# Layer 3 of a four-layer convolution block: two buffers for a block's v in the projections, and another order of the first key rows' loads

## The chip, the core and the metric

The kernel runs on one core of a Trainium2 chip, and the whole computation is one launch. The metric is the device time in microseconds (us), as the median of several executions. The engines are named as the profile names them: PE is TensorE's matmul side and PEld its weight load, DVE is VectorE, ACT is ScalarE, POOL is GpSimd and SP is SyncE, which here does nothing but issue transfers (DMAs).

## What is computed

The input `x` has 4 images of 256 channels on a 48x48 grid, float32. Four layers follow one another, each of the form "x plus a function of the group-normalised x". Cut to what matters here:

```python
x = x + _L0_conv_ref(_gn(x), ...)   # 7x7 dilated convolution -> softmax over 49 taps -> weighted sum of shifted x
x = x + _L1_conv_ref(_gn(x), ...)   # 3x3 convolution of signs
x = x + _L2_conv_ref(_gn(x), ...)   # 3x3 convolution with ternary weights
x = x + _L3_conv_ref(_gn(x), L3_conv_Wq, L3_conv_Wk, L3_conv_Wv, L3_conv_Wout, L3_conv_bout)

def _L3_conv_ref(x, Wq, Wk, Wv, Wout, bout):      # HEADS = 8, d = 32
    q = einsum('bchw,oc->bohw', x, Wq); k = ...Wk; v = ...Wv      # 1x1 projections, 8 heads of 32
    q = sigmoid(q); k = sigmoid(k)
    v = v / maximum(norm(v, axis=1), 1e-12)                       # per head and position
    ...
    for w in (1, 2, 4):     # windows of 48, 24 and 12 rows and columns round each position
        attn = q . (sum over the window of k v)  /  (q . (sum over the window of k) + 1e-6)
    return Wout . concatenate(outs) + bout
```

So layer 3 is linear attention over three square windows. The kernel computes it as scores (q times k), times a mask for each window, times v.

## The kernel before

The kernel works image by image through layers 0 to 2. Layer 3 cannot begin before image 0 has passed layer 2. Its projections for image 0 are interleaved with the last image's layers 0 to 2, as a "filler"; the attention of layer 3 begins after that. The projections of images 1 to 3 are interleaved with the attention of the image before.

A projection is done by groups: a group is one block of 8 rows (there are NRB = 6 blocks in an image, and NKC = 3 column tiles in a block). This is the part that makes v of a block. `take` and `free` are counters of the program that writes the instructions; they decide the order of instructions, not waits on the chip. Waits on the chip come from the buffers: an instruction that writes a buffer waits until the last user of that buffer is done, and where that user is a transfer, until it has landed. Every engine executes its instructions in the order in which they are written here.

```python
free = {"xr": 2, "xn": 2, "kt": 2, "sq": 2, "vt": 1, "cs": 1, "o": 1, "rc": 2, "res": 2}
...
def v(self, g, a, c):                       # group g, block of rows a, column tile c = 0, 1, 2
    ...
    if c == 0:
        yield from take("vt")
        self.vs[g] = (
            self.scr.tile([P, NKC, HEADS, D], F32, tag="vt", name="vt", bufs=1),
            self.scr.tile([P, NKC, HEADS], F32, tag="ss", name="ss"),
        )
    vt, ss = self.vs[g]
    yield from bank(1)
    ps = self.ps_tile()[:, 0:C].rearrange("p (h d) -> p h d", d=D)
    for ct in range(NCT):
        pe.matmul(ps, self.xn[g][:, ct, c, :], proj["v"][:, ct, :], start=(ct == 0), stop=(ct == NCT - 1))
    self.used(g)
    yield 1
    act.copy(vt[:, c], ps)                  # ACT empties the PSUM bank into vt
    yield 1
    yield from take("sq")
    sq = self.scr.tile([P, HEADS, D], F32, tag="sq", name="sq")
    pool.tensor_mul(sq, vt[:, c], vt[:, c])
    yield 2
    dve.tensor_reduce(ss[:, c, :], sq, AX.X, ALU.add)
    free["sq"] += 1
    if c < NKC - 1:
        return
    ...                                     # 1/norm of each head: ACT square root, DVE reciprocal and a Newton step
    dve.tensor_mul(vt, vt, r...)            # normalised in place
    yield 1
    sync.dma_start(out=v_d[b][:, a * NKC : (a + 1) * NKC], in_=vt)
    free["vt"] += 1
    made.add(("v", b, a))
```

The class `Projection` is used twice: with the pool `scr0` for image 0 (opened with two buffers for each name, and two PSUM tiles), and with the pool `scr` inside layer 3 for images 1 to 3 (also two buffers for each name). `bufs=1` overrides that for `vt`.

```python
def project_first():                        # the filler during the last image's layers 0 to 2
    scr, ps = (first.enter_context(tc.tile_pool(name=name, bufs=2, side="right", **kwargs))
               for name, kwargs in (("scr0", {}), ("ps_0", {"space": PSUM})))
    ...
    groups = [(a, ("k0", "v", "q0")) for a in range(NRB)]
    groups += [(a, ("k1", "q1")) for a in range(NRB)]
    proj["first"] = Projection(0, scr, ps, "ps", [P, 512]), groups
    start(paced(proj["first"][0].groups(groups), 1))
    while active:
        advance()
        yield 1.2
```

Layer 3's attention takes the tiles of keys for one block of query rows in an order that alternates near and far rows. One tile is a pair (block of key rows a, column tile c). The scores of a tile need `ks` of its row block; its sums, written LAG = 2 tiles later, need `vs` of it.

```python
def load_kv(b, ct, a):
    ks = kvp.tile([P, NKC, P], F32, tag="ks", name="ks")
    sync.dma_start(out=ks..., in_=k_d[b][chans, cols])
    vs = kvp.tile([P, NKC, HG, D], F32, tag="vs", name="vs")
    sync.dma_start(out=vs, in_=v_d[b][:, a * NKC : (a + 1) * NKC, ct * HG : (ct + 1) * HG, :])
    kvs[b, ct, a] = ks, vs

def tiles_of(rb):
    tiles = [(a, c) for a in sorted(range(NRB), key=lambda a: abs(a - rb)) for c in (1, 0, 2) if seen(0, a, rb)]
    near = [t for t in tiles if seen(NW - 1, t[0], rb)]
    far = [t for t in tiles if t not in near]
    both = min(len(near), len(far))
    return [t for pair in zip(near, far) for t in pair] + near[both:] + far[both:]
    # for rb = 0: (0,1) (2,1) (0,0) (2,0) (0,2) (2,2) (1,1) (3,1) (1,0) (3,0) (1,2) (3,2)
...
seen_first = HALVES[0] // RB + 1            # 4
until(("q", 0, 0, 0), ...)                  # q, k and v of these rows are written
qs = {0: load_q(*order[0])}
for a in range(seen_first):                 # 0, 1, 2, 3
    load_kv(0, 0, a)
...
for n in range(len(stream) + LAG):          # the attention's main loop, one tile after the other
    ...
        ss = [blocks[i].scores(pr, a, c) for pr in range(NPR)]      # PE, two PSUM tiles of the pool's two
        ahead.append(blocks[i].masked(a, c, ss))                    # DVE, ACT and POOL empty and mask them
    ...
```

The output projection's weights `wout_sb` (768 KB) are loaded once, by a transfer that ACT issues at the beginning of layer 3.

Of the kernel before, what the change touches and what calls it, by code (L numbers as in the profile page):

```python
# [12 lines left out]
F32 = mybir.dt.float32  # L13
# [8 lines left out]
P = 128  # L22
# [52 lines left out]
HEADS, D = 8, 32  # L75
# [4 lines left out]
NKC = W // KC  # L80
# [65 lines left out]
def conv_preact_kernel(  # L146
# [113 lines left out]
    def bank(steps):  # L260

        nonlocal bank_free
        while step < bank_free:
            yield 1
        bank_free = step + steps
# [6 lines left out]
    def take(what):  # L272
        while free[what] == 0:
            yield 1
        free[what] -= 1
# [11 lines left out]
    class Projection:  # L287
# [84 lines left out]
        def v(self, g, a, c):  # L372
            b = self.b
            while g not in self.xn or (c > 0 and g not in self.vs):
                if g in self.left:
                    return
                yield 1
            if c == 0:
                yield from take("vt")
                self.vs[g] = (  # L380
                    self.scr.tile([P, NKC, HEADS, D], F32, tag="vt", name="vt", bufs=1),
                    self.scr.tile([P, NKC, HEADS], F32, tag="ss", name="ss"),
                )
            vt, ss = self.vs[g]
# [3 lines that stand above are left out]
                pe.matmul(  # L388
                    ps,
                    self.xn[g][:, ct, c, :],  # L390
                    proj["v"][:, ct, :],
                    start=(ct == 0),
                    stop=(ct == NCT - 1),
                )
            self.used(g)
            yield 1
            act.copy(vt[:, c], ps)
# [10 lines that stand above are left out]
            n = NKC * HEADS  # L408
            t = ss.rearrange("p k h -> p (k h)")
            r, s, u = (small.tile([P, n], F32, tag=f"{x}{n}", name=x) for x in ("vr", "vs", "vu"))  # L410
            dve.tensor_scalar_max(t, t, 1e-24)
            yield 1
            act.activation(s, t, AF.Sqrt)
            yield 1
            dve.reciprocal(r, s)
            dve.tensor_mul(u, t, r)
            dve.tensor_mul(u, u, r)
            dve.tensor_scalar(u, u, -0.5, 1.5, ALU.mult, ALU.add)
            dve.tensor_mul(r, r, u)
            dve.tensor_mul(  # L420
                vt,
                vt,
                r.rearrange("p (k h) -> p k h", h=HEADS)
                .unsqueeze(3)
                .to_broadcast([P, NKC, HEADS, D]),
# [5 lines that stand above are left out]
# [21 lines left out]
    with (  # L452
# [50 lines left out]
        class Stats:  # L503
# [8 lines left out]
            def end(self, wait):  # L512
                mv = small.tile([P, NCT, 2], F32, tag="gn_mv", name="gn_mv")
                for ct in range(NCT):
                    dve.bn_aggr(mv[:, ct, :], self.st[:, ct])
                m = small.tile([P, NCT], F32, tag="gn_m", name="gn_m")
                v = small.tile([P, NCT], F32, tag="gn_v", name="gn_v")
                r = small.tile([P, NCT], F32, tag="gn_r", name="gn_r")
                wait(1.5)
                ps = ps_st.tile([P, NCT], F32, tag="st", name="gn_ps")  # L520
                pe.matmul(ps, gmat, mv[:, :, 0], start=True, stop=True)
                dve.tensor_copy(m, ps)

                dve.tensor_sub(v, mv[:, :, 0], m)
                dve.tensor_mul(v, v, v)
                dve.tensor_add(v, v, mv[:, :, 1])
                wait(2.5)
                ps = ps_st.tile([P, NCT], F32, tag="st", name="gn_ps")
                pe.matmul(ps, gmat, v, start=True, stop=True)
                dve.tensor_scalar_add(v, ps, GN_EPS)  # L530
                rsqrt(r, v, NCT)
                return m, r
# [848 lines left out]
        with tc.tile_pool(name="wst", bufs=1) as wst:  # L1381
# [18 lines left out]
            for ct in range(NCT):  # L1400
                for k0, k1 in TAPS:
# [3 lines left out]
                    else:  # L1405
                        pool_, tag = {
                            (0, 0): (xp, "x1_0"),
                            (0, 2): (xp, "x1_1"),
                            (1, 0): (wst, "raw1"),
                            (1, 2): (wst, "raw"),  # L1410
                        }[ct, k0]
# [70 lines left out]
    with (  # L1482
# [168 lines left out]
        def load_kv(b, ct, a):  # L1651

            chans, cols = slice(ct * P, (ct + 1) * P), slice(a * NB, (a + 1) * NB)
            ks = kvp.tile([P, NKC, P], F32, tag="ks", name="ks")
            sync.dma_start(out=ks.rearrange("p k n -> p (k n)"), in_=k_d[b][chans, cols])
            vs = kvp.tile([P, NKC, HG, D], F32, tag="vs", name="vs")
            sync.dma_start(
                out=vs, in_=v_d[b][:, a * NKC : (a + 1) * NKC, ct * HG : (ct + 1) * HG, :]
            )
            kvs[b, ct, a] = ks, vs  # L1660

        def load_q(b, ct, rb):
            qs = qp.tile([P, RB, W], F32, tag="qs", name="qs")
            sync.dma_start(
                out=qs.rearrange("p r w -> p (r w)"),
                in_=q_d[b][ct * P : (ct + 1) * P, rb * NB : (rb + 1) * NB],
            )
            return qs
# [158 lines left out]
        def seen(wi, a, rb):  # L1827
            r0, r1 = rows_seen(wi, a, rb)
            return r0 < r1

        def tiles_of(rb):


            tiles = [
                (a, c)
                for a in sorted(range(NRB), key=lambda a: abs(a - rb))
                for c in (1, 0, 2)
                if seen(0, a, rb)
# [5 lines that stand above are left out]
# [84 lines left out]
        seen_first = HALVES[0] // RB + 1  # L1928
        until(("q", 0, 0, 0), *((what, 0, *at) for a in range(seen_first) for what, at in (("k", (0, a)), ("v", (a,)))))
        qs = {0: load_q(*order[0])}  # L1930
        for a in range(seen_first):
            load_kv(0, 0, a)


# [53 lines left out]
        for n in range(len(stream) + LAG):  # L1988
            if n < len(stream):
                i, a, c, at, last = stream[n]  # L1990
# [6 lines left out]
            if n >= LAG:  # L1997
                i, a, c, at, last = stream[n - LAG]
# [57 lines left out]
```

## Time and profile before

| | before |
|---|---|
| time, median of 3 runs (lowest to highest) | 3734.66 us (3732.04 to 3744.95) |
| span of the profiled execution | 3730.0 us |
| granted PE clock, mean | 0.954 |
| instructions | 69121 |

Where these parts lie in the span, with the busy time of the engines in each stretch:

| stretch, us | what runs | PE | DVE | ACT | POOL | PE clock |
|---|---|---|---|---|---|---|
| 1160 to 1300 (140) | last image's layer 0, second half, with image 0's projections | 98.81 | 43.40 | 68.90 | 12.04 | 0.79 |
| 1300 to 1430 (130) | last image's layers 1 and 2, remaining projections, first tiles of layer 3 | 105.89 | 74.55 | 29.29 | 32.17 | 0.90 |
| 1430 to 3050 (1620) | layer 3's attention of images 0 to 2, with projections of images 1 to 3 | 1458.27 | 1132.04 | 579.13 | 1066.85 | 0.97 |
| 3050 to 3730 (680) | the rest of layer 3 | 646.04 | 433.35 | 208.84 | 304.34 | 0.99 |

How to read it. The busy time of an engine beside the length of a stretch tells how near that engine is to setting the pace there; it doesn't tell which wait ends last. In the timeline, one line is a run of like instructions: start, length, engine, operation, then what is written and what is read, and in square brackets the time for which the engine stood idle before it, with the event that ended the idle time. "DMA v_d<-vt" as such an event means that the transfer from `vt` to the scratch tensor `v_d` had landed. A line for "SPq" is the issue of a transfer, not its landing. All lines name L142 because a helper issues every operation, so groups are told apart by the names of their tiles.

### The profile page before, as it was taken

How to read it: one execution, taken by the hardware profiler on the slowest of the kernel's cores; microseconds unless marked ns; L12 is line 12 of the kernel's file. 1: busy time of each engine (PE TensorE's matmuls, PEld its weight loads, DVE VectorE, ACT ScalarE, POOL GpSimd, SP SyncE). 2: the span in 40 equal slices, each digit the busy share in tenths (PEclk: the TensorE clock that was granted, in tenths of full speed). 3: DMA queues.
4: the chain of work that ended last, by engine and by line, in shares of the span. 5: the costliest groups of instructions: out<-in, count | busy, mean ns of one | idle time of the engine just before them, and what ended most of it. 6: DMA issues, size and time to landing. Idle time of an engine off the chain costs nothing. (4 is left out here: it accounts for less than half of the span.)

```text
span 3730.0 us, 69121 instructions
## 1 busy us (share of the span) xinstructions
PE 3284.1 (88%) x26498; PEld 1873.8 (50%) x26498; DVE 2494.9 (67%) x5059; ACT 1067.4 (29%) x2085; POOL 1528.0 (41%) x2184
## 2 busy tenths in 40 slices
PE   3689998998996788988899888999999899999998
PEld 2467686686784664433334333344444344444443
DVE  7876587586583266778667466866577866666665
ACT  0012111111114422443222334333344422333331
POOL 0000120120030024788765476866366766344442
PEclk9789999999997899999899999999999999999999
DMA  7745333324314323345344253434222444200222
GB/s 251 225 143 184 101 108 120 105 98 125 107 65 124 117 70 98 119 140 168 105 133 134 74 151 109 154 99 136 75 94 87 153 124 124 70 31 31 65 60 60
DMA packets 373020, 423.04 MB, mean 113 GB/s; under 512 B 129076, under 2 KB 328532, under 8 KB 371540
## 3 DMA queue, kind: packets, MB, share of 16 engines
q1 hardware_dynamic: 371491, 416.32, 36.2%
q8 instruction: 211, 3.46, 0.4%
q0 software_dynamic: 144, 1.52, 0.2%
q14 instruction: 118, 0.96, 0.1%
q10 hardware_dynamic: 1056, 0.79, 0.1%
HBM read 288.79 MB, written 131.25 MB: 113 GB/s over the span
## 5 line engine op out<-in xcount | busy, mean ns | idle before, releaser
L142 DVE TENSOR_TENSOR sm<-s,masks 128x112 f32<-128x112 f32 (+10 forms) x2592 | 1149.2, 492 | 704.7 <-ACT sm L142 297.1
L142 POOL TENSOR_TENSOR sm<-sm,masks 128x432 f32<-128x432 f32 (+14 forms) x1152 | 883.1, 788 | 900.9 <-ACT sm L142 397.5
L142 ACT COPY sm<-s 128x528 f32<-128x528 f32 (+2 forms) x1152 | 588.3, 534 | 1423.0 <-PE s L142 1281.9
L142 PE MATMUL s<-qs,ks 32*128 32x320 f32 (+3 forms) x5760 | 859.7, 499 | 127.8 <-ACT sm L142 65.2
L142 PE MATMUL acc<-sm,vs 128*32 128x384 f32 (+18 forms) x13440 | 879.5, 384 | 21.5 <-POOL sm L142 21.2
L142 PEld LDWEIGHTS s<-qs,ks 32*128 32x128 f32 x5760 | 372.0, 185 | 558.3 <-DVE sm L142 225.1
L142 PE MATMUL cv<-vx,wt 128*128 128x288 f32 x2080 | 561.1, 426 | 92.5 <-DVE vx L142 50.7
L142 PEld LDWEIGHTS acc<-sm,vs 128*32 128x32 f32 x13440 | 355.0, 110 | 555.0 <-issue 327.0
L142 PEld LDWEIGHTS cv<-vx,wt 128*128 128x128 f32 x2080 | 403.5, 198 | 213.8 <-issue 55.2
L142 POOL MEMSET v<- 128x16 f32 (+1 forms) x120 | 18.5, 214 | 722.1 <-DVE vx L142 628.5
L142 PE MATMUL cv<-v,wl 128*128 128x384 f32 x1152 | 222.2, 352 | 24.3 <-DVE x L142 9.2
L142 PEld LDWEIGHTS cv<-v,wl 128*128 128x128 f32 x1152 | 212.7, 193 | 34.0 <-issue 15.8
L142 POOL TENSOR_TENSOR pt<-pt 128x144 f32<-128x144 f32 x336 | 180.4, 537 | 22.3
L142 POOL TENSOR_TENSOR v<-l2v,v 128x384 fp32r<-128x384 f32 x96 | 109.0, 1164 | 127.0 <-ACT v L142 118.3
L142 POOL TENSOR_TENSOR nhi<-nhi,nq 128x384 f32<-128x384 f32 x144 | 147.9, 1055 | 0.0
L142 PE MATMUL cv<-pad,wl 128*128 128x384 bf16 x864 | 143.1, 327 | 0.0
L142 PE MATMUL out_ps<-o,wout_sb 128*128 128x384 f32 x288 | 123.7, 512 | 11.2 <-DMA rc<-r_d 5.7
L142 DVE TENSOR_TENSOR pt<-cs 128x384 f32<-128x384 f32 x144 | 119.2, 827 | 0.0
L142 PE MATMUL out_ps<-stage,wout_sb 128*128 128x384 f32 x288 | 118.6, 494 | 0.5 <-DVE stage L142 0.5
L142 DVE TENSOR_TENSOR vx<-v 128x868 f32<-128x868 f32 x112 | 115.3, 1055 | 0.5
L142 PE MATMUL proj_ps<-wv_sb,xn 128*128 128x256 f32 x288 | 88.3, 434 | 29.3 <-ACT vt L142 19.3
L142 PEld LDWEIGHTS <-wl 128*128 128x128 bf16 x864 | 83.8, 97 | 59.1 <-issue 0.4
(162 smaller groups left out, 2881.3 us busy)
## 6 DMA issues: line engine op xcount, KB each, us to landing
wt<-wt SPq DMA_DIRECT2D x48, 768.0 KB
kb_d<-pt SPq DMA_DIRECT2D x48, 576.0 KB
rc<-r_d SPq DMA_DIRECT2D x192, 144.0 KB
nhi<-kb_d SPq DMA_DIRECT2D x120, 192.0 KB
nlo<-kb_d SPq DMA_DIRECT2D x88, 192.0 KB
o_d<-stage SPq DMA_DIRECT2D x24, 576.0 KB
o<-o_d SPq DMA_DIRECT2D x24, 576.0 KB
wl<-wl_d SPq DMA_DIRECT2D x16, 768.0 KB
```

The source lines that it names most:

```text
L142: return lambda *args, **kwargs: self.tc.keep_in_program_order(op(*args, **kwargs))
```

## The change

Two edits. The first drops `bufs=1` for `vt`, so that it has its pool's two buffers, in the projections of image 0 and in those of images 1 to 3: a group's first copy into `vt` need no longer wait for the landing of the previous group's transfer out of it. The counter `free["vt"]` stays at 1. The second fetches the first four blocks of key rows in the order in which the first block's tiles use them, 0, 2, 1, 3 where it was 0, 1, 2, 3.

```diff
             if c == 0:
                 yield from take("vt")
                 self.vs[g] = (
-                    self.scr.tile([P, NKC, HEADS, D], F32, tag="vt", name="vt", bufs=1),
+                    self.scr.tile([P, NKC, HEADS, D], F32, tag="vt", name="vt"),
                     self.scr.tile([P, NKC, HEADS], F32, tag="ss", name="ss"),
                 )
@@
         qs = {0: load_q(*order[0])}
-        for a in range(seen_first):
+        for a in dict.fromkeys(a for a, _ in tiles_of(0)):
             load_kv(0, 0, a)
```

## The prediction

> **What bounds the kernel now.** I read the page's first part for the shares, then everything that touches `vt` (the views of that tile), then ACT's and PE's timelines round each wait found there, and last the timeline at the beginning of layer 3.
>
> ```profile
> PE 3284.1 (88%) x26498; PEld 1873.8 (50%) x26498; DVE 2494.9 (67%) x5059; ACT 1067.4 (29%) x2085; POOL 1528.0 (41%) x2184
> ```
>
> PE sets the pace over the whole, so what the change is worth is read from the time for which PE stands still because of the things it touches. The first edit removes only one kind of wait. The view of `vt` in the stretch 1160 to 1430, where image 0 is projected, shows all of it:
>
> ```profile
> L142 ACT COPY vt<-proj_ps x18: 348/372/392, 1162.6 to 1292.4; 128x256 f32<-128x256 f32 x18
>   DMA v_d<-vt: 21.1, 5
>   PEld proj_ps L142: 26.9, 7
>   PE proj_ps L142: 23.2, 5
> ```
>
> Six groups, so five times a group's first copy follows another group's transfer: five waits, 21.1 us in sum. The last two lines are who waited for those copies. The same view for 1430 to 1960 has one idle entry, `PE proj_ps` with 1.1 us, and those for 1960 to 2500 and 2500 to 3050 also show no wait for `v_d`. So in the attention's 18 groups the second buffer has nothing to remove, and the first edit lives from five places. ACT's timeline has them:
>
> ```profile
> 1186.27 0.65 ACT L142 COPY vt<-proj_ps 128x256 f32<-128x256 f32 x2 [5.11 <-DMA v_d<-vt]
> 1204.26 0.65 ACT L142 COPY vt<-proj_ps 128x256 f32<-128x256 f32 x2 [4.18 <-DMA v_d<-vt]
> 1225.13 0.37 ACT L142 COPY vt<-proj_ps 128x256 f32<-128x256 f32 x1 [2.94 <-DMA v_d<-vt]
> 1255.75 0.37 ACT L142 COPY vt<-proj_ps 128x256 f32<-128x256 f32 x1 [1.25 <-DMA v_d<-vt]
> 1283.54 0.37 ACT L142 COPY vt<-proj_ps 128x256 f32<-128x256 f32 x1 [7.61 <-DMA v_d<-vt]
> ```
>
> ACT is busy 68.90 of the 140 us there, so its waits matter only as far as PE stands behind them. PE's timeline of the same places:
>
> ```profile
> 1186.70 2.08 PE L142 MATMUL proj_ps<-wv_sb,xn 128*128 128x256 f32 x4 [6.89 <-ACT vt L142]
> 1204.69 2.07 PE L142 MATMUL proj_ps<-wv_sb,xn 128*128 128x256 f32 x4 [2.48 <-ACT vt L142]
> 1225.91 0.52 PE L142 MATMUL tra<-ident,rows 120*120 120x120 f32 x3 [1.10 <-ACT seen L142]
> 1256.18 1.13 PE L142 MATMUL proj_ps<-wv_sb,xn 128*128 128x256 f32 x4 [0.70 <-ACT vt L142]
> 1283.96 2.08 PE L142 MATMUL proj_ps<-wv_sb,xn 128*128 128x256 f32 x4 [7.28 <-ACT vt L142]
> ```
>
> The second edit is at the beginning of layer 3:
>
> ```profile
> 1416.24 1.66 PE L142 MATMUL s<-qs,ks 32*128 32x384 f32 x8
> 1416.50 0.42 ACTq L1494 DMA_DIRECT2D wout_sb<-in_wout_dram  x1
> 1417.20 0.48 SPq L142 DMA_DIRECT2D ks<-k_d  x1
> 1424.55 1.78 PE L142 MATMUL s<-qs,ks 32*128 32x384 f32 x8 [6.64 <-DMA ks<-k_d]
> ```
>
> The second tile needs row block 2, whose `ks` is the third to be issued (at 1417.20) and is there 7.3 us later. PE stands for 6.64 us, and by then ACT, DVE and POOL have run dry too.
>
> **What the Trainium skill says.** "Perfetto Trace Analysis", Optimization Strategy, says that a bubble that returns on the engine that should be saturated can come from too few buffers. The trace agrees: five waits, each at a group's first copy. "DMA: Bandwidth & Descriptors", Queues, rings and completion order, says that one issuer's descriptors are consumed in ring order and that a DMA engine alternates between issuers' rings by packets. The packet records agree: of the 1536-byte packets (`ks`) row block 1's end at about 1418.4 and row block 2's at about 1423.0, while 512-byte packets (`vs`) and 1024-byte ones (`wout_sb`) run mixed between. So exchanging two loads in SP's ring exchanges their landings. "TensorE: Matmul & The Clock Gate", Part 1, says that PE's clock falls to half after some idle time and returns after sustained work. The trace agrees as far as it goes: the mean granted clock is 0.66 in 1280 to 1300, after the idle 7.28 us, 0.50 in 1415 to 1430 and 1.00 in 1300 to 1332.
>
> **The change part by part.** No instruction is added or removed, and as the counter for `vt` stays at 1, their order is the same but for the two exchanged loads. `vt` takes 3 x 8 x 32 x 4 = 3072 bytes per partition, once more in each of two pools; later tiles of these pools move by that much.
>
> First edit, the five places. I take PE's idle time where the copy ends it, cut to what the landing causes:
> - 1186: the copy could go when ACT is free, at 1181.17 (its exponential from 1180.80 lasts 0.37), as its PSUM tile is full by 1179.8. It comes 5.11 us earlier, and PE, which waits 6.89, gains **5.1**. The matmuls of the last logits stand behind it, so the whole chain of layer 0 moves.
> - 1204: the first v matmuls (start 1200.13, 2.08 us for two copies' worth) fill a bank at about 1201.2, so about 3 of the 4.18 are the landing's; PE idles 2.48, all removed: **2.5**.
> - 1225: PE waits 1.10 for `seen` behind the copy. A round trip from PE to ACT and back is there anyway (0.45 us at 1213.90): I take **0.5**.
> - 1256: **0.7**.
> - 1284: the transfer was issued at 1275.21 behind four weight loads (1270.87 on). The copy also holds up the reciprocal root of layer 1's statistics, at 1285.22 with its input there since about 1277, and the rows of `pad` that layer 1's matmuls need. Layer 1 begins at 1296.39 and moves with it: **7.3**.
>
> Sum 16.1 us. Against it, waits that can step in: ACT's `sg` waits for the landing of `q_d` once for 1.58 us and for 0.38 us, `xn` needs its rows, and `band_d` held DVE's `spread` for 2.1 us. They were hidden in part behind these stalls. I subtract 3 (an estimate: roughly one of these waits again at two of the three big places). **First edit: 13.**
>
> Second edit: row block 2 takes the place of row block 1, so its last packet is at 1418.4 where it was at 1423.0. PE came 1.5 us after the last packet (1424.55), so it would be allowed at about 1420. The scores also need both PSUM tiles emptied: DVE's masks of the first tile run from 1417.98 for 2.28 us, to 1420.26, and ACT's second copy ends at 1419.81. So the scores start at about 1420.3, which is **4.2** us earlier, and the wait left (2.4 us behind DVE) takes the place of the one removed. Row block 1 is then needed by the seventh tile; even at 1424.5 it is there before that. `vs` of row block 2, needed two tiles later, takes the landing of the old `vs` 1 (last packet at about 1422.2), in time.
>
> Clock: shorter idle stretches leave PE less often at half speed. The half-speed stretch from 1281.92 lasts 13.65 us in the trace's clock records, with some 7 us of work in it; the one from 1415.04 lasts 17.07. I add **2**, the vaguest term.
>
> In all 13 + 4 + 2 = 19, and 3734.7 - 19 = 3715.7: I predict **3716 us**.
>
> **The rivals.**
> 1. Another wait takes the place (gain 5 to 10, time 3725 to 3730). ACT has table loads of 1.28 us between its functions in this stretch, two `sg` buffers with transfers of their own, and PE waits 11.4 us for `sg` in 1160 to 1350. For it: these queues are as tight as `vt`. Against it: in each of the three big places the wait was for `vt` alone by 2.5 to 7.3 us, and the transfers that `sg` waits for were issued well before (1183.86, read next at 1194.41).
> 2. The gain is hidden: PE loses it again further on, because the weights of layers 1 and 2 land no earlier. For it: 2.7 MB of weight loads are in flight from 1270.87, at 350 to 430 GB/s. Against it: layer 1's are first in the ring, a quarter of those bytes, some 2 us of traffic, and the start would move only to about 1280. Layer 1 runs with no idle time from 1296.39 for 35.78 us, so from there a shift stays a shift. If true for that place: time about 3723.
> 3. The moved tiles (3 KB further) come to lie on memory that is released later, or the two stretches run at another granted clock. Nothing in the profile speaks for it: the tiles of keys come before the moved pool and the first masks have time. It would cost a few us either way: 3720 to 3737.
>
> **Range and chances.** If rival 1 and 2 both hold, the first edit is worth about 4 and the second 3: 3728. If nothing steps in and the clock gives 6, 16 + 4 + 6 = 26: 3709. The three runs before differ by 13 us, so the range is a little wider on each side: 3705 to 3730. Two per cent are 74.7 us; the whole of the waits concerned is 28 us (21.1 + 6.64). So within 2% is nearly sure: 0.97, faster by more 0.02, slower by more 0.01.
>
> **What would show it.** In the changed profile: no wait of ACT `vt` for `v_d`; layer 1's first long run of `cv` (1296.39 before) at about 1283, which is the first edit's 16 less the 3, give or take the clock; the second tile's scores after an idle time of about 2.4 us that DVE's `sm` ends. From about 1440 on every stage is to have the length it had. The prediction is wrong if the run of `cv` starts after 1290 (then ACT's other waits have stepped in), if the second tile still waits for `ks`, or if the length of the attention from there to the end differs by over 5 us, which neither edit accounts for.

## The result, and the profile after

The changed kernel takes 3714.77 us (median of 4 runs, 3709.3 to 3717.27) where the kernel before took 3737.36 in the runs beside it: a ratio of 0.9936 (95% interval 0.9914 to 0.9958). Measured once more on another chip it is 3715.24 us and 0.9931 (0.9912 to 0.9950). So some 23 to 26 us are gone, within 2%, and near the 3716 us predicted; but the sum behind that number has one term that was far too small, and it lacks a loss that came.

The first line of the page of the changed kernel, busy time by engine: PE's busy time is what it was (3284.1 before), in a span that is 14.5 us shorter in this one execution. That sum hides that PE is faster in one stretch and slower in others; the stretches below tell.

```profile
PE 3283.8 (88%) x26498; PEld 1871.7 (50%) x26498; DVE 2493.9 (67%) x5059; ACT 1067.6 (29%) x2085; POOL 1530.5 (41%) x2184
```

The view of `vt` in image 0's projections, 1140 to 1420: what ended the idle time ahead of its instructions, and who waited for it.

```profile
L142 ACT COPY vt<-proj_ps x18: 350/371/378, 1164.1 to 1272.2; 128x256 f32<-128x256 f32 x18
  ACT vt L142: 100.6, 13
  DVE ss L142: 17.4, 3
  PE proj_ps L142: 2.1, 2
  DVE vr L142: 0.2, 1
...
  PEld proj_ps L142: 9.9, 4
  PE proj_ps L142: 7.3, 2
```

The entry for `v_d` (21.1 us before) is gone. Of the 7.3 us for which PE still waits for a copy, 6.53 are at 1271.69, where ACT first writes layer 1's input (5.86 us at 1291.89 before). PE's timeline of the changed kernel at the places that the prediction went through:

```profile
1182.96 2.07 PE L142 MATMUL proj_ps<-wv_sb,xn 128*128 128x256 f32 x4 [0.73 <-ACT vt L142]
...
1199.23 1.78 PE L142 MATMUL proj_ps<-xn,wk_sb 128*128 128x384 f32 x4 [0.80 <-ACT xn L142]
1200.85 1.45 PE L142 MATMUL proj_ps<-xn,wq_sb 128*128 128x384 f32 x4
1202.14 0.37 PE L142 MATMUL tra<-ident,rows 120*120 120x120 f32 x2
...
1276.97 36.07 PE L142 MATMUL cv<-pad,wl 128*128 128x384 bf16 x216
...
1397.82 1.66 PE L142 MATMUL s<-qs,ks 32*128 32x384 f32 x8
1401.45 2.19 PE L142 MATMUL s<-qs,ks 32*128 32x384 f32 x8 [1.97 <-ACT sm L142]
```

The first line stood at 1186.70 after 6.89 us of idle time. Layer 1's run of `cv` starts at 1276.97 where it was 1296.39. The second tile's scores wait 1.97 us, for ACT's copy, where they waited 6.64 us for `ks`. Two stretches serve from here on. **S1** runs from the second v projection of the second group (1178.68 before, 1180.16 after) to the run of `cv`; **S2** from the first scores to the zeroing matmuls ahead of the first sums. "The rest" is from those to PE's last matmul. The stretches view, S1 before and after (length, then busy us of PE, PEld, DVE, ACT, POOL, then clock, DMA share, GB/s):

```profile
1178.68:1296.39 117.71, 82.50 (x401) 63.16 (x402) 34.38 (x109) 53.41 (x95) 10.26 (x19) 0.77 0.41 128
```

```profile
1180.16:1276.97 96.81, 77.69 (x400) 60.53 (x401) 34.65 (x109) 54.09 (x96) 10.43 (x19) 0.82 0.49 155
```

S1 lost 20.9 us, S2 went from 13.13 to 8.49, and the rest grew from 2295.9 to 2304.5.

### The profile page after: what moved, and what is told of

The parts are those of the page before. It is cut to its first block, busy times and chain, and to the rows that moved or that the text cites. A ratio compares the mean times of both kernels' runs of the same rounds, so it can differ in the third digit from the quotient of the medians.

```text
span 3715.5 us, 69111 instructions
## 1 busy us (share of the span) xinstructions
PE 3283.8 (88%) x26498; PEld 1871.7 (50%) x26498; DVE 2493.9 (67%) x5059; ACT 1067.6 (29%) x2085; POOL 1530.5 (41%) x2184
## 5 line engine op out<-in xcount | busy, mean ns | idle before, releaser
L142 DVE SCALAR_TENSOR_TENSOR x<-cv,alpha,x 128x384 f32<-128x384 f32 x144 | 83.9, 609 | 43.3 <-PE cv L142 43.0
```

The source lines that it names most:

```text
L142: return lambda *args, **kwargs: self.tc.keep_in_program_order(op(*args, **kwargs))
```

## The experiments

All are compared with the kernel before on their own chip. First each edit alone, then the first edit in one of its two pools, then its memory without its effect.

**The first edit alone**

```diff
-                    self.scr.tile([P, NKC, HEADS, D], F32, tag="vt", name="vt", bufs=1),
+                    self.scr.tile([P, NKC, HEADS, D], F32, tag="vt", name="vt"),
```

> The first edit alone (two buffers for vt in both pools, loads in the old order 0, 1, 2, 3). Two stretches are measured in the trace. S1: from the start of the second v projection after 1178 us (before: 1178.68) to the start of layer 1's run of cv (before: 1296.39), 117.7 us before and 96.8 us with the whole change. S2: from the first scores (before: 1416.24) to the zeroing matmuls ahead of the first sums (before: 1429.37), 13.1 us before and 8.5 us with the whole change. Theory (the two edits act apart, each where its own wait was): S1 about 97, S2 about 13, time about 18 us (14 to 21) under before. Rival (the earlier end of layer 2 also changes what is in flight at the start of layer 3): S2 differs from 13.1 by over 2 us.

3711.78 us, ratio 0.9916 (0.9903 to 0.9930). S1 is 90.4, S2 13.4, the rest 2295.2. The edit acts in S1 alone, but takes more than expected: about 28 us between the medians and 31 by the ratio, as much as the whole change or more.

```profile
1186.72:1277.13 90.41, 69.75 (x400) 53.66 (x401) 34.70 (x109) 54.06 (x96) 10.62 (x19) 0.92 0.54 166
```

**The second edit alone**

```diff
-        for a in range(seen_first):
+        for a in dict.fromkeys(a for a, _ in tiles_of(0)):
             load_kv(0, 0, a)
```

> The second edit alone (one buffer for vt, loads in the order 0, 2, 1, 3). Theory: S1 as before, 117 to 118; S2 about 8.5; the second tile's scores wait about 2 us for ACT or DVE and not for ks; time 4 to 5 us under before. Rival (the gain at the start of layer 3 is taken back in the attention, where PE is not the only one that sets the pace): S2 8.5 but time within 1.5 us of before.

3732.85 us, ratio 0.9980 (0.9972 to 0.9988): about 7 us. S1 123.8, S2 8.4, the rest 2291.6, so nothing was taken back. The wait left at the second tile is as long as expected, but is put down to `ks` here, which came about when ACT and DVE were done:

```profile
1431.74 1.94 PE L142 MATMUL s<-qs,ks 32*128 32x384 f32 x8 [2.20 <-DMA ks<-k_d]
```

**Two buffers in image 0's projections only**

```diff
-                    ... tag="vt", name="vt", bufs=1),
+                    ... tag="vt", name="vt", bufs=2 if self.tag == "ps" else 1),
```

> Two buffers for vt in image 0's projections alone; in layer 3's own projections one buffer as before, so no tile of the attention lies elsewhere than before. Theory (the attention's 18 groups have no such wait): as the first edit alone within 3 us, S1 about 97, time about 18 us under before. Rival (the second buffer also matters in the attention, for better or, by moving its tiles, for worse): differs from the first edit alone by over 5 us.

3712.2 us, ratio 0.9925 (0.9912 to 0.9937); S1 92.8, the rest 2295.4. That is the first edit alone within the intervals: no effect of the second buffer shows in the attention's 18 groups.

**One buffer, twice as wide**

```diff
-                    self.scr.tile([P, NKC, HEADS, D], F32, tag="vt", name="vt", bufs=1),
+                    self.scr.tile([P, 2 * NKC, HEADS, D], F32, tag="vt", name="vt", bufs=1)[:, 0:NKC],
```

> One buffer for vt, but twice as wide, its second half unused: the same memory as two buffers, with all tiles where the change has them, and the wait kept. Theory (the wait is what counts): S1 about 117.7, five waits of ACT's copies for v_d, time within 5 us of before. Rival (the gain comes from where the tiles lie, not from the wait): S1 near 97. If moved tiles cost something in the attention, as the 8.6 us by which the one changed profile is longer there could mean, this run is 5 to 9 us slower than before.

3741.12 us, ratio 1.0000 (0.9988 to 1.0012); S1 121.7, the rest 2294.7, and the wait is there in full:

```profile
  DMA v_d<-vt: 23.9, 5
```

With the old order of loads, no effect shows of where the tiles lie.

**One buffer, freed by DVE instead of by the landing**

```diff
-            dve.tensor_mul(vt, vt, r...)
+            vn = self.scr.tile([P, NKC, HEADS, D], F32, tag="vn", name="vn", bufs=1)
+            dve.tensor_mul(vn, vt, r...)
-            sync.dma_start(out=v_d[b][...], in_=vt)
+            sync.dma_start(out=v_d[b][...], in_=vn)
```

> One buffer for vt and the old order of loads, but DVE's normalisation writes into a separate tile, from which the transfer goes out; so vt is free for the next group when DVE has read it, and nobody waits for the landing but DVE's next normalisation. Theory (the landing is what was waited for): as the first edit alone, S1 90 to 97, no wait of ACT's copies for v_d, ratio about 0.992. Rival (a second buffer for vt is needed because the next group's copies come before the previous group is normalised): S1 stays over 110, with ACT's copies waiting for DVE.

3712.14 us, ratio 0.9927 (0.9909 to 0.9944); S1 96.7, no wait for `v_d`. The first copies of the second group go straight after the exponential, as with two buffers:

```profile
1185.49 0.37 ACT L142 ACTIVATE e<-e 120x196 f32<-120x196 f32 x1 [0.34 <-DVE e L142]
1185.77 0.63 ACT L142 COPY vt<-proj_ps 128x256 f32<-128x256 f32 x2
```

So the landing was the cause, not the number of buffers: one buffer that the transfer doesn't hold does the same.

**Matmuls that keep the clock up.** With the waits (four traces: before, the second edit alone, the wide buffer, and the late `wout_sb` below) S1 is 121.8 us in the mean: PE idle 37.1, busy 84.8. Without them (seven traces: the change twice, the first edit alone, image 0 only, freed by DVE, and two runs below) it is 92.9: idle 20.1, busy 72.8. The work is the same, so 12 of these 29 us are matmuls that run faster. Is that the clock? The clock records have PE at half speed for 62 us of S1 with the waits and 23 without. This run keeps all waits of the kernel before and fills PE's idle time at three of the five places with work that nobody uses.

```diff
+            if self.warm is not None:
+                self.warm(g, c)                  # ahead of the v projection's matmuls
+                def warm(g, c):
+                    n = {(1, 2): 28, (2, 1): 10, (2, 2): 8, (5, 2): 40}.get((g, c), 0)
+                    if n:
+                        w = ps_st.tile([P, P], F32, tag="st", name="warm")
+                        for _ in range(n):
+                            pe.matmul(w, ident, ident, start=True, stop=True)
```

> The kernel before, with 86 matmuls added that compute nothing used (128x128, float32, into a PSUM tile that nobody reads), placed ahead of the v projections of groups 1, 2 and 5, where PE stands waiting for ACT's copies: 28, 10 + 8 and 40 of them. All five waits stay. In the six traces so far PE's idle time in S1 is 37.1 us in the mean with the waits and 20.4 without, and its busy time 83.9 and 73.0, with half speed granted for 59.5 and 23.7 us. Theory (10.9 us of the gain is matmuls that run at full speed because PE stands idle for shorter): the added matmuls keep the clock up, half speed in S1 falls by 15 us or more, S1 falls by 3 to 8 us though no wait is taken away, and the copies still wait about 21 us for v_d. Rival (the busy time differs for another reason, or the idle time at ACT's own pace decides the clock): S1 121 or more.

3734.35 us, ratio 0.9988 (0.9978 to 0.9998): 3.4 us faster between the medians and 4.5 by the ratio, with more work and the same waits. ACT's copies wait 22.5 us for `v_d`, as before. S1 is 111.2, half speed 11.8 us.

```profile
1185.61 6.42 PE L142 MATMUL warm<-ident 128*128 128x128 f32 x56
...
1200.92 2.40 PE L142 MATMUL warm<-ident 128*128 128x128 f32 x20
...
1206.65 3.24 PE L142 MATMUL warm<-ident 128*128 128x128 f32 x16
...
1275.90 9.20 PE L142 MATMUL warm<-ident 128*128 128x128 f32 x80 [0.25 <-DVE gn_v L142]
```

```profile
1183.88:1295.10 111.22, 88.59 (x572) 73.80 (x573) 34.33 (x109) 53.86 (x95) 10.26 (x19) 0.95 0.44 135
```

The added matmuls take 21.3 us of the 88.6 busy, so the kernel's own take 67.3 where they take 82.5 to 87.2 in the traces with the waits. So it is the clock: PE's idle time costs itself, and then the slower matmuls after it. Not all that S1 gained stays in the time; the rest is 2299.4 in this trace, 3.5 more than before.

**Was `ks` late for its place, or for the bytes of `wout_sb`?** The kernel before, with that load moved.

```diff
-        nc.scalar.dma_start(out=wout_sb, in_=wout.rearrange("(kt p) o -> p kt o", p=P))
+            if i == 1:                           # at the second block of queries
+                act.dma_start(out=wout_sb, in_=wout.rearrange("(kt p) o -> p kt o", p=P))
```

> The kernel before, old order and one buffer, with the load of wout_sb (768 KB, issued by ACT at the start of layer 3) moved to the beginning of the second block of queries; it is first used five blocks later. The second edit took 4.7 us out of S2 by exchanging two loads. Question: was ks of row block 2 late for its place behind vs and ks of row block 1 alone, or for the bytes of wout_sb between? From the packets: ks of row block 1 ends at 1418.4; vs 1 and ks 2 are 393 KB, at the 250 to 300 GB/s seen there 1.4 to 1.6 us, so without wout_sb ks 2 would end at about 1420 instead of 1423.0. If the bytes count: the wait for ks falls from 6.6 to about 3.6 us and S2 from 13.1 to about 10. If the place alone counts: S2 stays at 13.

S2 is 10.3, as expected if the bytes count; the wait at the second tile fell to 4.14 us:

```profile
1429.32 1.77 PE L142 MATMUL s<-qs,ks 32*128 32x384 f32 x8 [4.14 <-DMA ks<-k_d]
```

So both count: about 2.9 us come from the weights in between (S2 is 12.3 to 13.5 in the six other traces with the old order), and the exchange of loads takes 4.7 with them still there. The time as a whole shows none of it: 3738.92 us, 1.0004 (0.9992 to 1.0015), with an S1 of 124.1 in the trace.

**The whole change again.** Between the medians, the parts alone add up to about 35 us, and the whole takes 23.

> The whole change once more, beside the kernels below on one chip. The first edit alone has come out at a ratio of 0.9916 and the second alone at 0.998, while the whole change was put at 0.9936, and its one trace is 9 us longer after the start of layer 3's sums (2304.5 us, against 2291.6 to 2295.9 in the five other traces). If the edits add up: ratio about 0.990, S1 about 93, S2 about 8.5, the rest 2291 to 2297. If together they cost something in the attention that neither costs alone: ratio 0.993 to 0.995 again and the rest about 2304 again.

Ratio 0.9931 (0.9912 to 0.9950), S1 90.2, S2 8.5 and the rest 2306.8. The loss is in the rest again.

**Both edits, the attention's tiles where they lay**

```diff
-                    ... tag="vt", name="vt", bufs=1),
+                    ... tag="vt", name="vt", bufs=2 if self.tag == "ps" else 1),
-        for a in range(seen_first):
+        for a in dict.fromkeys(a for a, _ in tiles_of(0)):
```

> Both edits, but in layer 3's own projections vt keeps one buffer, so that the attention's tiles lie where they lay before. Alone, the edits took 0.84% and 0.2%; together 0.69%, and in all three traces with both the time from the first zeroing matmuls to PE's last matmul is 2300 to 2307 us where seven traces without both have 2292 to 2299. Theory A ([...]where the tiles lie doesn't matter): the rest is 2300 to 2307 here too, ratio 0.992 to 0.994. Theory B (the moved tiles and the new order of loads get in each other's way): the rest is 2292 to 2297, ratio about 0.990.

3709.61 us, ratio 0.9918 (0.9902 to 0.9934), S1 90.2, S2 8.5, the rest 2300.0. Theory A is that the attention's work meets the stretches of half speed, which lie on a grid of 3.41 us in the clock records (last section), at another place of the grid, as the second edit takes 4.7 us out ahead of it. By the rest, moved tiles are not the whole cause (2292 to 2297 was expected then), but the ratio lies between the two expectations. Whether they are a part of it is open: this kernel is 6.8 us faster between the medians than the next one on the same chip, which has the moved tiles and 1 us of added matmuls.

**The whole change, shifted by three matmuls**

```diff
                 for acc in self.accs[1:]:
                     pe.matmul(acc, zeros[:, 0:P], zeros, start=True, stop=False)
+                if (self.b, self.ct, self.rb) == (0, 0, 0):
+                    for _ in range(3):
+                        pe.matmul(self.accs[1], zeros[:, 0:P], zeros, start=False, stop=False)
```

> The whole change, and three more zeroing matmuls ahead of the first sums (they add zeros), so PE and all behind it come some 1 us later from there. Theory A (phase against the clock windows): the rest changes by several us although the work is the same but for 1 us, and the half-speed stretch that the three traces with both edits have at 66 us after the zeroing (and the traces with one edit mostly don't) is gone or moves. Theory B: the rest stays 2300 to 2307, plus 1 us.

In the trace the half-speed stretch at 66 us after the zeroing is gone (the first one now is at 120, where before has it at 119) and the rest is 2299.8, but the time, 3716.45 us with 0.9940 (0.9922 to 0.9957), is no better than that of the whole change. A shift moves single stretches of half speed about; that this makes the loss is not shown, and the run freed by DVE speaks against it: it has the stretch at 65 us too, with a rest of 2296.8.

**A version that goes on: four buffers for `sg`.** On the whole change, in image 0's projections.

```diff
-            t = self.scr.tile([P, NB], F32, tag="sg", name="sg")
+            t = self.scr.tile([P, NB], F32, tag="sg", name="sg", bufs=4 if self.tag == "ps" else 2)
```

> The whole change, and four buffers for the sigmoid's output sg in image 0's projections where there were two. In the changed kernel ACT's sg waits until 1318.42 for the landing of q_d, whose issue SP could not reach because it was held by two weight loads (1295.26 for 18.13 us), and PE stands for 3.34 us behind it, with layer 2's statistics after that. Theory: this wait goes and layer 2 begins 3 to 4 us earlier (from the start of layer 1's run of cv to the first scores 117 us where it was 119.9 to 121.4); time 3 to 4 us under the whole change. Rival (another wait takes its place: kt, or the square roots of the statistics): unchanged within 1 us.

3704.45 us, ratio 0.9913 (0.9894 to 0.9931), beside 0.9931 for the whole change on the same chip. The medians differ by 10.8 us, more than the 3 to 4 expected, and the intervals of the ratios overlap. From the run of `cv` to the first scores the trace has 116.4 us where the changed kernel has 120.3 to 120.9: the same mechanism once more, ACT's sigmoid waiting for the landing of a transfer. ACT's timeline in the changed kernel and in this one:

```profile
1318.42 0.49 ACT L142 ACTIVATE sg<-proj_ps 128x384 f32<-128x384 f32 x1 [39.73 <-DMA q_d<-sg]
```

```profile
1310.14 0.49 ACT L142 ACTIVATE sg<-proj_ps 128x384 f32<-128x384 f32 x1 [34.82 <-PE proj_ps L142]
```

**The parts that were worth it together**

```diff
-            t = self.scr.tile([P, NB], F32, tag="sg", name="sg")
+            t = self.scr.tile([P, NB], F32, tag="sg", name="sg", bufs=4 if self.tag == "ps" else 2)
-                    ... tag="vt", name="vt", bufs=1),
+                    ... tag="vt", name="vt", bufs=2 if self.tag == "ps" else 1),
-        for a in range(seen_first):
+        for a in dict.fromkeys(a for a, _ in tiles_of(0)):
```

> Both edits with vt's second buffer in image 0's projections only, and four buffers for sg there. From the parts: the former came out at a ratio of 0.9918, and four buffers for sg took 4.5 us (120.9 to 116.4) from the stretch between layer 1's run of cv and the first scores. So a ratio of about 0.9906, 3702 us. The time from the zeroing matmuls to PE's last matmul is 2300 to 2307 in the five traces with both edits and 2292 to 2299 in eight without; if what costs these 6 us comes with both edits, it is 2299 or more here as well.

3699.55 us, ratio 0.9904 (0.9886 to 0.9921), the lowest of all, though the intervals of several others overlap it. S1 87.6, run of `cv` to the first scores 116.6, S2 8.5, the rest 2300.8, in the band of the other traces with both edits.

## Why the prediction was right

The time was right and the mechanism of both edits was right, but the split was not, and two errors of opposite sign helped the number. Step by step:

- **PE's idle time at the five places: 16.1 us predicted.** In S1 PE's idle time fell from 37.1 to 20.1, by 17.0 in the means over four and seven traces (35.2 to 19.1 in the first pair alone). In the one changed trace, counted along PE from its start of S1 (1.48 us later than before), the five steps are 5.2, 7.0, 0.9, 0.8 and 7.0 where 5.1, 2.5, 0.5, 0.7 and 7.3 were predicted. The second has a misreading in it: four lines of the v projection (x4) are one copy's worth, not two, so the bank was full at 1197.4 and the whole 4.18 us was the landing's. The rest of that step is the clock. PE's timeline before:

```profile
1196.35 1.03 PE L142 MATMUL proj_ps<-wv_sb,xn 128*128 128x256 f32 x4
...
1207.56 2.93 PE L142 MATMUL proj_ps<-xn,wk_sb 128*128 128x384 f32 x4 [0.80 <-ACT xn L142]
1210.28 2.77 PE L142 MATMUL proj_ps<-xn,wq_sb 128*128 128x384 f32 x4
```

- **Waits that step in: 3 us subtracted.** None shows. The drop in idle time is the full predicted sum, and the rival of another wait taking the place is refuted, as is the one of weights that land late: the run of `cv` came at 1276.97, not after 1290.
- **The clock: 2 us predicted, 12 measured** (84.8 to 72.8 us of busy time for the same work, in the means; in the first pair alone 4.8). This is the term that was badly mis-sized. The two projections ahead of the first `tra` took 2.93 and 2.77 us before and take 1.78 and 1.45 after. The trace of before has half speed for 54.6 us of S1; the prediction named one such stretch there, of 13.65 us, and put no price on the work in the others.
- **The second edit: 4.2 us predicted,** 4.6 to 4.7 in S2. The remaining wait was put at 2.4 us, behind DVE's masks, and is 1.97, behind ACT's copy: the scores start at 1401.45, while DVE's run of masks goes on to 1401.84.
- **"From about 1440 on every stage is to have the length it had": wrong.** Six traces with both edits have a rest of 2299.8 to 2306.8 us (mean 2302.0), eight traces without both have 2291.6 to 2299.4 (mean 2295.7). So 6.3 us are lost there in the means, more than the second edit gained; in the first changed trace it is 8.6, above the 5 us that the prediction named as a sign of being wrong. Each edit alone doesn't lose them, but the two bands nearly touch: the 2299.4 is the run with the added matmuls, which has neither edit. The place of the tiles isn't the whole cause, by two traces with both edits and the tiles where they lay (2300.0 and 2300.8). PE's busy time in the rest is 2106.6 us in the mean with both edits and 2103.2 without, at half speed for 118.5 and 110.8 us. So 3.4 of the 6.3 us are slower matmuls, and the other half is waiting. What ties the loss to both edits together stays open.

Summed by the means: 29 us from the first edit, 4.7 from the second, 6.3 back, 27 net, which the interval holds (0.9912 to 0.9950 are 33 to 19 us). By the times more is lost than by the traces: 35 us for the parts, 23 for the whole. The prediction's 13 + 4 + 2 = 19 missed the first edit by 14 with its clock: 10 for the clock, 3 for waits that did not step in, 1 for the idle time. The loss that nobody foresaw made up for a part of this. So that the number came out near was in part luck: without the loss, 33.7 us off the 3734.7 would be 3701, below the range of 3705 to 3730.

## What to carry to other kernels

A buffer that a transfer empties is busy until the transfer has landed; when an in-order engine writes it next, everything behind that instruction waits too. Look for "DMA out<-tile" as what ended the idle time ahead of a copy; a second buffer, or a tile of its own for what goes out, removed it here without one instruction more. Where the engine behind is PE, count the idle time and then the matmuls that run at half speed after it: here 17 us of idle time brought 12 us on top. And order loads by first use: exchanging two loads of one issuer took 4.7 us here.

## What the runs showed of the hardware

The same idle time can cost or not. In the attention PE waits 1.56 us for the same `sg` in the changed kernel and in that with image 0 only; after it the four lines of the projection take 2.93 us in the one and 1.56 in the other. PE's timeline of the changed kernel, then of the other:

```profile
1472.39 2.93 PE L142 MATMUL proj_ps<-xn,wq_sb 128*128 128x384 f32 x4 [1.56 <-ACT sg L142]
```

```profile
1475.58 1.56 PE L142 MATMUL proj_ps<-xn,wq_sb 128*128 128x384 f32 x4 [1.56 <-ACT sg L142]
```

The clock records have half speed in stretches of 3.41, 6.83, 10.24, 13.65 and 17.07 us, whole multiples of 3.41, and in each trace their edges lie on one grid of that step. In the changed kernel the pause falls into one step of the grid; in the other kernel an edge at 1474.50 divides it. The stretches view of two steps each, the changed kernel first (length, busy us of PE, PEld, DVE, ACT, POOL, clock, DMA share, GB/s):

```profile
1468.70:1472.11 3.41, 1.88 (x20) 0.78 (x16) 3.38 (x8) 3.35 (x5) 3.19 (x6) 1.00 0.26 91
1472.11:1475.53 3.42, 3.13 (x8) 1.45 (x12) 1.73 (x5) 0.83 (x2) 0.19 (x1) 0.50 0.93 279
```

```profile
1471.08:1474.50 3.42, 2.68 (x36) 1.13 (x28) 3.42 (x8) 2.94 (x5) 3.10 (x7) 1.00 0.02 9
1474.50:1477.91 3.41, 2.33 (x12) 0.99 (x12) 2.49 (x7) 1.61 (x3) 0.99 (x1) 1.00 0.96 279
```

PE idles for 1.53 us in one step, and the next is at half speed; or for 0.74 and 1.08 us in two, and the clock stays full. So in this pair it fits that idle time counts by steps of the grid. It gives no sharp limit: elsewhere in the changed kernel a step with 0.89 us idle was followed by half speed, and one with 1.99 was not.

And work that computes nothing can pay: 21.3 us of added matmuls made the kernel some 4 us faster (0.9988, 0.9978 to 0.9998).
